# Newton steps for the inverse roots of the expert tiles, constants and FP4 weight loads placed behind tiles, and a permutation inverted in bf16

## The chip, the cores and the metric

The kernel runs on one core of one Trainium2 chip. The metric is the device time in microseconds of one execution. The core has five engines, each with its own queue of instructions that it works off in order: PE (TensorE: matrix products and transposes), DVE (VectorE), ACT (ScalarE), POOL (GpSimd) and SP (SyncE, which here only issues transfers). Engines wait for each other through semaphores. Transfers between HBM and SBUF are issued from the queues of SP, ACT and POOL and are carried out by 16 DMA engines.

## The reference

Six layers work on x, 4 batches of 1024 tokens with 256 features in f32. They form two Macaron blocks; each layer adds its result to x:

```python
x = x + 0.5 * moe(layernorm(x))            # 4 experts, top 1, hidden size 1024
x = x + softmax_attention(layernorm(x))    # 16 heads of 16, causal
x = x + 0.5 * moe(layernorm(x))            # the same weights
x = x + 0.5 * fp4_ffn(layernorm(x))        # hidden size 704
x = x + linear_attention(layernorm(x))     # squared normalised features, running sums
x = x + 0.5 * fp4_ffn(layernorm(x))        # the same weights
```

The two layers that matter here:

```python
def moe(x):
    e = argmax(x @ W_router)                       # one expert per token
    h = gelu(x @ W1[e] + b1[e])
    y = h @ Wo + bo + x
    return (y - mean(y)) * rsqrt(var(y) + 1e-12) * gamma + beta

def fp4_quant_dequant(x):                          # blocks of 16 along the last axis
    scale = max(max(abs(xb)) / 6, 1e-12)
    return nearest of {0, .5, 1, 1.5, 2, 3, 4, 6} to abs(xb / scale), with its sign, times scale

def fp4_ffn(x):
    g, u = q(x) @ q(w_gate).T, q(x) @ q(w_up).T    # q is fp4_quant_dequant
    return q(silu(g) * u) @ q(w_down).T
```

## The kernel before, in words

x stays in SBUF for the whole kernel, as 8 blocks (`xb`) of 512 tokens, that is 128 partitions x 4 x 256. Six stages follow each other. In the profile of before they lie at about 0 to 507 us (MoE, phase 0), 507 to 1580 (softmax attention), 1580 to about 1990 (MoE, phase 1), then FP4, linear attention, and FP4 again until the end.

**Where the order comes from.** The source is written engine by engine, and the program is a trace of it. A scheduler then orders the instructions on each engine by its own estimates of their costs; in the two attention stages parts of PE's order are written out by hand. `tc.keep_in_program_order(ins)` tells the scheduler that `ins` must stand, in its engine's queue, behind everything that the source has given this engine before. It adds no semaphore and no wait of its own; it fixes a place in a queue. Since each queue is worked off in order, an instruction that waits holds back whatever stands behind it on its engine.

**The MoE phase** (`moe_phase`, L247) has three parts.

*Routing* (`moe_route`, L281), for each of the 8 blocks: the block is normalised (`norm_block`, L204: statistics on DVE at L210 and L211, the root on ACT at L213, its reciprocal on DVE at L215, the normalising on ACT at L220), stored to `xn_d` in HBM (L284), transposed on PE (L234) and copied (L235); 8 products with the router's weights give the logits (L292). DVE marks each token's expert in `hot` (L296 to L305), small products give each token's rank (place) among the tokens of its expert (L310 to L325), and then the permutation "token to rank" is turned around. For this the rank is split into a column c and a place q within 128 (L329 to L333). For each group of 128 tokens, `oc` marks the column and `oq` the place, with the token's number in place of a one (L337, L339; f32, 128x128), and the product of the two is summed over all 32 groups into a PSUM bank `inv` (L340). An f32 product is two records on PE. c and q come from adding and subtracting WHOLES = 1.5 * 2^23, which rounds an f32 number to a whole one; `c` keeps WHOLES added, and `alongm` is a row of counting numbers with WHOLES added.

*Plan* (`moe_plan`, L342): `inv` is copied to `invT` (L349); a product of it with a 0/1 matrix `pick` (L380, L382) picks, for each of 38 columns of 128 slots, the tokens to gather (`ids`); `w1_at` gives the rows of the expert's W1 to gather, and `y_at` where each token finds its result.

*Tiles* (`moe_tile`, L415): 19 tiles of 256 slots, each with one expert. POOL issues the gathers: W1 of the expert, 1 MB (L417; three buffers `w1`), and the tokens, two transfers (L422; three buffers `xg`). PE transposes the tokens (L428), ACT copies them (L430), POOL adds the bias bo to `xg` (L432). PE forms the hidden layer in two halves, in PSUM `pairA` and `pairB` (L440), ACT takes the gelu (L447), and PE multiplies by Wo into `acc` (L453). DVE adds `xg` (L456, the first to write y), `norm_block` normalises (L210, L211, L213, L215, L225), POOL multiplies by gamma (`gam0`, halved beforehand at L115) and adds beta (`bet0`, halved at L116) at L458 and L459, and SP stores y to `y_d` (L460). The root at L213 and the gelu at L447 need different tables on ACT, so ACT loads a table on each change between them. There is one `acc` bank; so the next tile's L453 waits until L456 has read it.

After the last tile, each token's result is gathered back and added to x (`give_back`, L274) at the beginning of the next stage.

**Work between the tiles.** `moe_phase` takes a generator `between` and calls `next(between)` after each tile. In phase 0 this is `fp4_weights` (L747): four steps that fill `vas` (128x4096, ones) and `low` (128x512, zeros) on POOL (L749), then 8 parts of w_gate and w_up, and two of w_down. Each part loads `raw` on SP (L755 of 88x512; L773 of 128x352, twice per part), quantises it (`fp4`, L709: L718 to L731 on DVE, with L728 on ACT, and L732 on POOL, which writes `q`), transposes q on PE (L761, L778) and copies the result on ACT (L764). `raw` has two buffers. In phase 1 the generator is empty. The scheduler may move all of this ahead in the queues, and does: the first `raw` is issued at 13.76 us.

**Constants** (L115 to L189): the halving of gam0 and bet0, the identity `ident` and its bf16 copy `ident16` (L122, a cast on DVE), masks for the attention stages (`mask_q`, `keep_kq`, `own`, and `parity` and `row16`, taken from them by DVE at L152 and L154), counting rows (L164, L166), `alongm` (L171), and the `eps` columns that ACT's root takes as a bias (L185, L187).

Of the kernel before, what the change touches and what calls it, by code (L numbers as in the profile page):

```python
# [10 lines left out]
F32 = mybir.dt.float32  # L11
BF16 = mybir.dt.bfloat16
U32 = mybir.dt.uint32
AF = mybir.ActivationFunctionType
# [3 lines left out]
P = 128  # L18
# [24 lines left out]
def macaron_kernel(  # L43
# [38 lines left out]
    def acc_bank(shape):  # L82
        return psum.tile(shape, F32, tag="acc", name="acc", bufs=1)
# [28 lines left out]
    for b in range(2, NBLK):  # L112
        load_x(b)

    nc.gpsimd.tensor_scalar(gam0, gam0, 0.5, None, ALU.mult)  # L115
    nc.gpsimd.tensor_scalar(bet0, bet0, 0.5, None, ALU.mult)  # L116


    ident = const.tile([P, P], F32, tag="ident", name="ident")
    make_identity(nc, ident)  # L120
    ident16 = const.tile([P, P], BF16, tag="ident16", name="ident16")
    nc.vector.tensor_copy(ident16, ident)  # L122
# [4 lines left out]
    nc.gpsimd.memset(mask_q, 0.0)  # L127
    make_causal_mask(nc, mask_q[:, BLK - P :], mask_val=NEG)

    keep_kq = const.tile([P, P], F32, tag="keep_kq", name="keep_kq")  # L130
    nc.gpsimd.memset(keep_kq, 1.0)
    nc.gpsimd.affine_select(
        out=keep_kq, in_=keep_kq, compare_op=ALU.is_ge, fill=0.0, base=0, pattern=[[1, P]], channel_multiplier=-1
    )

    own = const.tile([P, 2, 8, HD + 1], F32, tag="own", name="own")
    nc.gpsimd.memset(own, 1.0)
    for step, base, cm in ((-HD, 0, 1), (HD, HD - 1, -1)):
        nc.gpsimd.affine_select(
            out=own,  # L140
            in_=own,
            compare_op=ALU.is_ge,
            fill=0.0,
            base=base,
            pattern=[[0, 2], [step, 8], [0, HD + 1]],
            channel_multiplier=cm,
        )

    parity = const.tile([P, 2], F32, tag="parity", name="parity")
    own_par = own.rearrange("p g (h two) c -> p g two h c", two=2)  # L150
    for i in range(2):
        nc.vector.tensor_reduce(parity[:, i : i + 1], own_par[:, 0, i, :, 0], AX.X, ALU.add)  # L152
    row16 = const.tile([P, 1], F32, tag="row16", name="row16")
    nc.vector.tensor_reduce(row16, ident.rearrange("p (j c) -> p j c", c=32)[:, :, HD], AX.X, ALU.add)  # L154
# [14 lines left out]
    along = counting("along", [P], 0, [[1, P]], 0)  # L169
    alongm = const.tile([P, P], F32, tag="alongm", name="alongm")  # L170
    nc.vector.tensor_scalar(alongm, along, WHOLES, None, ALU.add)  # L171
    token = counting("token", [TT], 0, [[P, TT]], 1)
# [11 lines left out]
    eps5 = const.tile([P, 1], F32, tag="eps5", name="eps5")  # L184
    nc.gpsimd.memset(eps5, 1e-5)  # L185
    eps12 = const.tile([P, 1], F32, tag="eps12", name="eps12")
    nc.gpsimd.memset(eps12, 1e-12)  # L187
# [10 lines left out]


# [4 lines left out]
    def norm_block(dst, src, eps, last=None):  # L204
# [7 lines left out]
        std = small.tile([P, TPB], F32, tag="std", name="std")  # L212
        nc.scalar.activation(std[:, 0:n], mv[:, 0:n, 1], AF.Sqrt, bias=eps)  # L213
        rstd = small.tile([P, TPB], F32, tag="rstd", name="rstd")
        nc.vector.reciprocal(rstd[:, 0:n], std[:, 0:n])  # L215
# [31 lines left out]
    def moe_phase(tag, between):  # L247
# [4 lines left out]
        with tc.tile_pool(name=f"moe{tag}", bufs=2, reuse_waits="tile") as wp, tc.tile_pool(  # L252
# [6 lines left out]
            inv = acc_bank([P, P])  # L259
# [3 lines left out]
            wf0 = load(f0_wo, "wf0", nc.scalar, sp)  # L263
            for s in range(NE):
                moe_tile(wp, s, xn_d, y_d, wf0, w1_at, ids, b1s)
                next(between, None)
# [14 lines left out]
    def moe_route(wp, b, xn_d, hot, ranks, inv):  # L281
# [48 lines left out]
        nc.vector.tensor_scalar(c, c, WHOLES, None, ALU.add)  # L330
        q = small.tile([P, TPB], F32, tag="q", name="q")
        nc.vector.tensor_scalar(q, c, WHOLES, float(-P), ALU.subtract, ALU.mult)
        nc.vector.tensor_tensor(q, q, r, ALU.add)  # L333
        for i in range(TPB):
            t = b * TPB + i
            oc = wp.tile([P, P], F32, tag="oc", name="oc", bufs=TPB)
            nc.vector.tensor_scalar(oc, alongm, c[:, i : i + 1], None, ALU.is_equal)  # L337
            oq = wp.tile([P, P], F32, tag="oq", name="oq", bufs=TPB)
# [408 lines left out]
    def fp4_weights(wp):  # L747
        for t in (*vas, *low):
            nc.gpsimd.memset(t, 1.0 if t in vas else 0.0)  # L749
            yield  # L750
# [372 lines left out]
```

## Time and profile before

| what | us |
|---|---|
| runs shown | 3208.11, 3191.23, 3205.8 |
| their median | 3205.8 |
| the profiled execution | 3201.22 |
| its span | 3199.5 |
| PE busy | 2630.5 |
| DVE busy | 1565.7 |
| ACT busy | 1036.2 |
| POOL busy | 684.6 |

The profile is of one execution, and its span is the time from the first to the last instruction; 1.7 us of the execution lie around it. Engines work at the same time, so their busy times don't add up to the span. The granted clock of PE, as a share of full speed, is 0.89 in the mean.

In a timeline each row has the start, the time that it took, the engine, the line of the source, the operation, out<-in with the sizes, and how many instructions the row takes together (x4). In brackets stands how long the engine had been idle before, and what it was waiting for. "PEld" is the loading of weights on PE, which runs beside the products. "SPq" and "POOLq" are the issuing of transfers; their time is the engine's, not the transfer's.

The beginning of y (L456) marks the pace of the tiles. Its starts in phase 0, in us: 119.06, 135.51, 158.30, 179.77, 202.47, 223.98, 246.86, 268.24, 289.19, 312.03, 331.81, 348.45, 364.82, 381.20, 397.64, 415.11, 434.26, 450.20, 466.14. In phase 1: 1665.69, 1684.61, 1701.02, 1717.40, 1735.63, 1752.01, 1768.35, 1786.47, 1802.94, 1819.24, 1838.38, 1854.80, 1871.22, 1889.38, 1905.86, 1923.39, 1942.94, 1958.88, 1974.82.

### The profile page before, as it was taken

The page shows a single profiled execution, that of the slowest core. Times are in us where ns is not written, and L with a number is a line of the kernel's source. Part 1 is how long each engine was busy: PE and PEld are TensorE (multiplying, and loading weights), DVE is VectorE, ACT ScalarE, POOL GpSimd, SP SyncE. Part 2 cuts the span into 40 slices and gives each one's busy share as a digit, 9 for nine tenths or more (in the row PEclk, how much of TensorE's full clock was granted, in tenths as well). Part 3 has the DMA queues.
Part 4 walks back from the last instruction along what each step waited for, and adds up shares of the span by engine and source line. Part 5 has one row for each costly group of instructions (what it writes and reads, how often), then busy time and mean ns, then how long its engine had stood idle before and what let it go on. Part 6 is the DMA issues. An engine that isn't in the chain of part 4 may idle for free.

```text
span 3199.5 us, 35882 instructions
## 1 busy us (share of the span) xinstructions
PE 2630.5 (82%) x13697; PEld 1674.4 (52%) x13697; DVE 1565.7 (49%) x3877; ACT 1036.2 (32%) x1704; POOL 684.6 (21%) x760
## 2 busy tenths in 40 slices
PE   6878879998899899899788986678877888777887
PEld 5666754433433343333477775455654555445565
DVE  6233117555445544445231112986446665695644
ACT  3233431333333323333434342233222323232222
POOL 1333323101001001101023342421113322211111
PEclk8789996989889989989869998889988998988898
DMA  4322211000000000000122222100000000000000
GB/s 150 104 75 85 96 41 48 1 1 1 1 1 1 1 1 1 1 1 1 40 96 96 96 86 72 30 7 1 0 0 1 1 1 1 1 7 14 9 12 14
DMA packets 43556, 95.59 MB, mean 30 GB/s; under 512 B 4888, under 2 KB 32056, under 8 KB 38136
## 3 DMA queue, kind: packets, MB, share of 16 engines
q0 software_dynamic: 12192, 58.21, 5.7%
q1 hardware_dynamic: 30280, 32.58, 3.0%
q10 hardware_dynamic: 912, 2.51, 0.3%
q8 instruction: 108, 1.77, 0.2%
q14 instruction: 64, 0.52, 0.1%
HBM read 70.73 MB, written 22.54 MB: 29 GB/s over the span
## 4 chain that ended last, share of the span: by engine, by line
PE 51%; DVE 21%; issue 11%; POOL 7%; DMA 5%; ACT 4%; POOLq 0%; ACTq 0%; DVEq 0%
PE bank L590 11%; PE acc L838 5%; PE acc L652 5%; PE pairA L668 4%; PE bank L565 4%; DMA xg<-xn_d,ids 3%; PE acc L453 3%; POOL hq L732 2%; PE pairA L807 2%; PE pairB L807 2%; DVE sc L965 2%; PE bank L894 2%; DVE part L600 2%; PE pairB L440 1%; PE bank L834 1%
## 5 line engine op out<-in xcount | busy, mean ns | idle before, releaser
L590 PE MATMUL bank<-kT,qT 32*128 32x512 f32 (+3 forms) x1536 | 455.5, 603 | 38.4 <-DVE part L600 18.2
L590 PEld LDWEIGHTS bank<-kT,qT 32*128 32x128 f32 x1536 | 192.8, 206 | 269.4 <-DVE low L605 117.7
L678 ACT ACTIVATE ex<-pairA 128x1024 f32<-128x1024 f32 x192 | 155.5, 810 | 517.3 <-PE bank L590 200.7
L681 POOL TENSOR_SCALAR_AFFINE_SELECT ex<-ex 128x256 f32<-128x256 f32 x256 | 103.3, 408 | 917.4 <-ACT ex L678 913.6
L453 PE MATMUL acc<-wf,gT 128*128 128x256 f32 x1216 | 288.0, 386 | 0.0
L456 DVE TENSOR_TENSOR y<-acc,xg 128x512 f32<-128x512 f32 x38 | 26.3, 692 | 478.7 <-issue 337.9
L453 PEld LDWEIGHTS acc<-wf,gT 128*128 128x128 f32 x1216 | 236.5, 194 | 33.9
L668 PE MATMUL pairA<-qT,kT 32*128 32x512 f32 (+3 forms) x768 | 227.0, 579 | 2.2 <-ACT ex L678 2.2
L838 PE MATMUL acc<-wdT,hqT 128*128 128x256 f32 x768 | 222.0, 448 | 8.2 <-ACT hqT L835 5.4
L600 DVE TENSOR_REDUCE part<-bank 128x1 f32<-128x512 f32 x256 | 168.6, 687 | 76.5 <-PE bank L590 56.9
L668 PE MATMUL pairB<-qT,kT 32*128 32x512 f32 (+3 forms) x768 | 203.0, 576 | 0.0
L838 PEld LDWEIGHTS acc<-wdT,hqT 128*128 128x128 f32 x768 | 170.6, 230 | 50.8 <-ACT hqT L835 22.9
L834 PE MATMUL bank<-ident,hq 128*128 128x128 f32 x384 | 73.5, 345 | 145.7 <-POOL hq L732 145.7
L440 PE MATMUL pairB<-xgT,w 128*128 128x256 f32 x608 | 174.0, 413 | 23.3 <-ACT gT L447 23.3
L605 DVE CUSTOM_DVE_ANT_0 seen<-bank,mask_q 128x128 bf16<-128x128 f32 (+3 forms) x256 | 116.0, 489 | 154.5 <-PE bank L590 147.1
L732 POOL TENSOR_TENSOR hq<-hv,ham 128x1408 f32<-128x1408 f32 x32 | 83.1, 2596 | 496.2 <-DVE hv L731 449.6
L652 PE MATMUL acc<-ex,va 128*32 128x512 f32 (+3 forms) x1536 | 185.4, 550 | 0.9 <-POOL ex L681 0.4
L440 PE MATMUL pairA<-xgT,w 128*128 128x256 f32 x608 | 168.6, 402 | 11.9 <-ACT gT L447 10.5
L807 PE MATMUL pairA<-wgT,xqT 128*128 128x352 f32 x512 | 166.9, 469 | 3.1 <-ACT xqT L235 3.1
L605 DVE CUSTOM_DVE_ANT_0 seen<-bank,mask_q,part 128x128 bf16<-128x128 f32 (+3 forms) x256 | 131.1, 547 | 73.4 <-PE bank L590 62.1
L807 PE MATMUL pairB<-wuT,xqT 128*128 128x352 f32 x512 | 163.1, 461 | 2.6 <-DVE h L817 2.5
L447 ACT ACTIVATE gT<-pairA,b1s 128x256 f32<-128x256 f32 x152 | 71.8, 472 | 276.9 <-PE pairA L440 276.4
(249 smaller groups left out, 4696.0 us busy)
## 6 DMA issues: line engine op xcount, KB each, us to landing
y_d<-y SPq DMA_DIRECT2D x38, 256.0 KB, 2.1
xn_d<-xn SPq DMA_DIRECT2D x16, 512.0 KB, 2.8
x<-in_x SPq DMA_DIRECT2D x8, 512.0 KB, 9.7
out<-x SPq DMA_DIRECT2D x32, 128.0 KB, 1.7
wf<-in_f_wo ACTq DMA_DIRECT2D x2, 1024.0 KB, 9.4
xg<-xn_d,ids POOLq DMA_INDIRECT x76, 2.8
wqk<-in_a_wqk SPq DMA_DIRECT2D x1, 1024.0 KB
back<-y_d,y_at POOLq DMA_INDIRECT x64, 2.7
```

Of the source, the lines that this page charges most:

```text
L440: nc.tensor.matmul(pg[:, f, :], lhsT=w1[:, k * FF + fc * P : k * FF + (fc + 1) * P], rhs=xgT[:, k, :], start=(k == 0), stop=(k == KD - 1),)
L453: nc.tensor.matmul(po[:, j, :], lhsT=gT[fc][:, bass.ts(j, P)], rhs=wf0[:, fc, :], start=(fc == 0), stop=(fc == NF - 1))
L565: nc.tensor.matmul(pp, lhsT=wqk0[:, k, which, g, :], rhs=xnT[:, hb, k, :], start=(k == 0), stop=(k == KD - 1),)
L590: nc.tensor.matmul(pss[j][:, 0:n], lhsT=qT[rows, bass.ts(qt, P)], rhs=kT[rows, c * BLK : c * BLK + n], start=True, stop=True,)
L600: nc.vector.tensor_reduce(part[:, h : h + 1], pss[j][:, 0:n], AX.X, ALU.max, negate=True)
L605: nc.vector.tensor_tensor_reduce(out=seen[:, 0:n], in0=pss[j][:, 0:n], in1=mask_q[:, BLK - n : BLK], scale=-1.0, scalar=part[:, h : h + 1] ...
L652: nc.tensor.matmul(acc[qb][bass.ts(h, 32), c0:BLK], lhsT=va[:, kt, NG * g + h, :], rhs=exs[h // 2][:, h % 2, c0:BLK], start=(kt == 0), sto ...
L668: nc.tensor.matmul(pss[h // 2][:, h % 2, c0:BLK], lhsT=kT[rows, bass.ts(kt, P)], rhs=qT[rows, qb * BLK + c0 : (qb + 1) * BLK], start=True, ...
L678: nc.scalar.activation(ex[:, :, c0:BLK], ps[:, :, c0:BLK], AF.Exp, scale=0.25)
L732: mul.tensor_tensor(dst, v, am.unsqueeze(2).to_broadcast([parts, n, QB]), ALU.mult)
L807: nc.tensor.matmul(pg[:, half, 0:FIH], lhsT=xqT[:, k, bass.ts(i, P)], rhs=w[:, k, half * FIH : (half + 1) * FIH], start=(k == 0), stop=(k ...
L838: nc.tensor.matmul(po, lhsT=hqT[:, c, :], rhs=wdT[:, c, :], start=(c == 0), stop=(c == NFI - 1))
```

## The change

1. *Newton steps.* In the expert tiles, `norm_block` takes the inverse root on DVE by a new function `inverse_roots`: eps is added, a first guess comes from the bits of the number (times -0.5, plus a constant, on its int32 view), and three Newton steps of three operations follow; 11 small DVE operations in all. ACT's root and DVE's reciprocal are left out there. Routing and the other layers keep the root on ACT.
2. *Constants later.* The masks, `parity`, `row16` and the fills of `vas` and `low` move into a generator `later_constants`, from which `fp4_weights` yields first, so that they stand behind tiles 0 to 3, pinned; the fills are on DVE now, not on POOL. `ident16`, `alongm` and `eps12` are gone, `eps5` comes first, and the halving of gam0 and bet0 moves behind the plan of phase 0.
3. *FP4 weights.* The loads of `raw` are pinned on SP, each behind what SP was given before it.
4. *Permutation in bf16.* `oc` and `oq` are bf16. A token's number, up to 4095, is written as two numbers that bf16 holds exactly, the row (0 to 127) and the group (0 to 31), so `oq` is 128x2x128, one product per group of 128 tokens gives both sums, and the plan puts them together (copy, then one DVE operation that adds 128 times the group).
5. *Buffers.* `xg` has four buffers, not three.

The diff, cut (removed lines of constants that appear again in `later_constants` are left out; lines of the file after the change are 37 to 39 higher from `moe_tile` on, so L440 becomes L479, L453 L492, L456 L495, L761 L798 and L778 L815):

```diff
-    nc.gpsimd.tensor_scalar(gam0, gam0, 0.5, None, ALU.mult)
-    nc.gpsimd.tensor_scalar(bet0, bet0, 0.5, None, ALU.mult)
+    eps5 = const.tile([P, 1], F32, tag="eps5", name="eps5")
+    nc.gpsimd.memset(eps5, 1e-5)
...
-    nc.vector.tensor_copy(ident16, ident)
...
-    along = counting("along", [P], 0, [[1, P]], 0)
-    nc.vector.tensor_scalar(alongm, along, WHOLES, None, ALU.add)
-    token = counting("token", [TT], 0, [[P, TT]], 1)
+    along = const.tile([P, P], BF16, tag="along", name="along")
+    nc.gpsimd.iota(along, pattern=[[1, P]], base=0, channel_multiplier=0, ...)
+    token = const.tile([P, TT, 2], BF16, tag="token", name="token")
+    for i in range(2):
+        nc.gpsimd.iota(token[:, :, i], pattern=[[i, TT]], base=0, channel_multiplier=1 - i, ...)
+    row1 = counting("row1", [1], 0, [[1, 1]], 1)
...
+    def later_constants():
+        pinned = tc.keep_in_program_order
+        pinned(nc.gpsimd.memset(mask_q, 0.0))
+        make_causal_mask(nc, mask_q[:, BLK - P :], mask_val=NEG)
+        pinned(nc.gpsimd.memset(keep_kq, 1.0))
...
+        pinned(nc.gpsimd.memset(own, 1.0))
...
+        pinned(nc.vector.tensor_reduce(row16, ident.rearrange("p (j c) -> p j c", c=32)[:, :, HD], AX.X, ALU.add))
+        for t in (*vas, *low):
+            pinned(nc.vector.memset(t, 1.0 if t in vas else 0.0))
+            yield
...
+    def inverse_roots(dst, src, eps):
+        n = src.shape[1]
...
+        nc.vector.tensor_scalar(v, src, eps, None, ALU.add)
+        nc.vector.tensor_scalar(y.bitcast(I32), v.bitcast(I32), -0.5, float(0x5F3759DF), ALU.mult, ALU.add)
+        for step in range(3):
+            nc.vector.scalar_tensor_tensor(u, y, -0.5, y, ALU.mult, ALU.mult)
+            nc.vector.tensor_tensor(u, u, v, ALU.mult)
+            nc.vector.scalar_tensor_tensor(dst if step == 2 else y, u, 1.5, y, ALU.add, ALU.mult)

-    def norm_block(dst, src, eps, last=None):
+    def norm_block(dst, src, eps, last=None, roots=None):
...
+        if roots is nc.vector:
+            inverse_roots(rstd[:, 0:n], mv[:, 0:n, 1], eps)
+        else:
+            std = small.tile([P, TPB], F32, tag="std", name="std")
+            nc.scalar.activation(std[:, 0:n], mv[:, 0:n, 1], AF.Sqrt, bias=eps)
+            nc.vector.reciprocal(rstd[:, 0:n], std[:, 0:n])
...
-            inv = acc_bank([P, P])
+            inv = acc_bank([P, 2, P])
...
         nc.vector.tensor_scalar(c, c, WHOLES, None, ALU.add)
+        nc.vector.tensor_scalar(c, c, WHOLES, None, ALU.subtract)
...
-        nc.vector.tensor_scalar(q, c, WHOLES, float(-P), ALU.subtract, ALU.mult)
-        nc.vector.tensor_tensor(q, q, r, ALU.add)
+        nc.vector.scalar_tensor_tensor(q, c, float(-P), r, ALU.mult, ALU.add)
...
-            nc.vector.tensor_scalar(oc, alongm, c[:, i : i + 1], None, ALU.is_equal)
+            nc.vector.tensor_scalar(oc, along, c[:, i : i + 1], None, ALU.is_equal)
-            oq = wp.tile([P, P], F32, tag="oq", name="oq", bufs=TPB)
-            nc.vector.tensor_scalar(oq, along, q[:, i : i + 1], token[:, t : t + 1], ALU.is_equal, ALU.mult)
+            oq = wp.tile([P, 2, P], BF16, tag="oq", name="oq", bufs=TPB)
+            nc.vector.scalar_tensor_tensor(
+                oq, along.unsqueeze(1).to_broadcast([P, 2, P]), q[:, i : i + 1],
+                token[:, t, :].unsqueeze(2).to_broadcast([P, 2, P]), ALU.is_equal, ALU.mult)
             nc.tensor.matmul(inv, lhsT=oc, rhs=oq, start=(t == 0), stop=(t == TT - 1))
...
-        nc.scalar.copy(invT, inv)
+        nc.scalar.copy(invT, inv[:, 0, :])
+        nc.vector.scalar_tensor_tensor(invT, inv[:, 1, :], float(P), invT, ALU.mult, ALU.add)
...
-        xg = wp.tile([P, nj, D], F32, tag="xg", name="xg", bufs=3)
+        xg = wp.tile([P, nj, D], F32, tag="xg", name="xg", bufs=4)
...
-        norm_block(y, y, eps12)
+        norm_block(y, y, 1e-12, roots=nc.vector)
...
-        for t in (*vas, *low):
-            nc.gpsimd.memset(t, 1.0 if t in vas else 0.0)
-            yield
+        yield from later_constants()
...
-                nc.sync.dma_start(out=raw, in_=src[:, part * 2 * D : (part + 1) * 2 * D])
+                tc.keep_in_program_order(nc.sync.dma_start(out=raw, in_=src[:, part * 2 * D : (part + 1) * 2 * D]))
...
-                nc.sync.dma_start(out=raw, in_=f1_wd[:, a * FI + c0 : a * FI + c0 + FIH])
+                tc.keep_in_program_order(nc.sync.dma_start(out=raw, in_=f1_wd[:, a * FI + c0 : a * FI + c0 + FIH]))
```

## The prediction

> **What bounds the kernel now.** I read the page's totals first, then sums over stretches of time, then the timeline of the stretches that the diff touches.
>
> ```profile
> span 3199.5 us, 35882 instructions
> PE 2630.5 (82%) x13697; PEld 1674.4 (52%) x13697; DVE 1565.7 (49%) x3877; ACT 1036.2 (32%) x1704; POOL 684.6 (21%) x760
> ```
>
> PE is busy for 82% of the span. The two attention stages and the FP4 layers contain no edited instruction, so I ask only about the two MoE phases. The sums by stretch (start:end, length, busy time of each engine, clock):
>
> ```profile
> 200.00:340.00 140.00, 112.32 (x483) 91.35 (x482) 52.30 (x105) 53.67 (x96) 52.73 (x48) 0.91 0.25 82
> 340.00:456.00 116.00, 101.82 (x462) 84.91 (x462) 17.95 (x56) 47.69 (x81) 38.88 (x36) 0.99 0.23 73
> 1642.00:1965.00 323.00, 281.76 (x1248) 234.02 (x1249) 48.50 (x149) 129.83 (x222) 121.98 (x111) 0.95 0.28 92
> ```
>
> The first holds expert tiles with a part of the FP4 weight preparation in each (PE 80%), the second tiles of phase 0 without one (88%), the third the tiles of phase 1 (87%). So PE sets the pace everywhere, and a change pays or costs by the time for which PE stands still. One FP4 tile in detail, on the timeline:
>
> ```profile
> 223.98 0.69 DVE L456 TENSOR_TENSOR y<-acc,xg 128x512 f32<-128x512 f32 x1 [9.16 <-PE acc L453]
> ...
> 225.39 1.28 ACT L213 ACT_TABLE_LOAD   x1
> ...
> 231.01 1.27 POOL L458 TENSOR_TENSOR y<-y,gam 128x512 f32<-128x512 f32 x1
> ...
> 233.98 0.36 SPq L460 DMA_DIRECT2D y_d<-y  x1
> 234.43 0.37 SPq L755 DMA_DIRECT2D raw<-in_f_wu  x1
> ...
> 235.46 2.08 PE L440 MATMUL pairB<-xgT,w 128*128 128x256 f32 x4 [3.16 <-ACT gT L447]
> ```
>
> The reader should see two things. SP takes the store of y 10.0 us after DVE began on it, and a raw FP4 load 0.45 later; this raw is for a part several tiles ahead (the first was issued at 13.76, during routing), so nobody waits for it. And PE's loss is 3.16 us, behind a gelu queued on ACT after an FP4 step.
>
> **The change, part by part.** *Raw loads pinned on SP.* A pinned instruction stands behind all that the program gave its engine before. In the queues of the built program SP now has, for ten tiles: store of y (tile s), raw load, store of y (tile s+1), and so on. DVE has: normalise y of tile s, FP4 of that raw part, y of tile s+1. PE has: the tile's last L492, the transposes of the quantised q (L798, or L815 for wd), and only then the transposes and products of tile s+1. So the whole chain from PE's last product to q lies on PE's path, where before it ran beside it. Step by step, from PE's end as zero:
> - y starts at 0.05; sum and statistics end 1.69 later (223.98 to 225.67): 1.74.
> - Newton: 11 dependent small operations. Those at 64.06, 64.27, 64.47, 64.68 follow each other by 0.205: 2.26. To 4.00. The old way took 1.55 (225.67 to 227.22), so this costs 0.7 here.
> - normalise 0.73; POOL's gamma and beta 1.34 and 1.27 (469.22, 470.56, 471.83): 7.4. Store, then raw 0.45 later: 7.9.
> - raw lands 2.65 after its issue, as the next rows show: 10.6.
>
> ```profile
> 299.28 4.65 SPq L773 DMA_DIRECT2D raw<-in_f_wd  x2
> ...
> 301.93 0.52 DVE L718 TENSOR_REDUCE wam<-raw 128x22 f32<-128x352 f32 x1 [1.13 <-DMA raw<-in_f_wd]
> ```
>
> - FP4 of 88x512: 0.68+0.15+0.35+0.68+0.42 on DVE (40.95 to 43.02), 0.72 on ACT, 0.69+0.69 on DVE, hand-overs 0.4: to 15.3. q on POOL 1.05 (228.38): 16.4.
> - PE then, cold: four transposes 0.8, four of xg 1.09 and 0.68 until the product (1646.45 and 1648.22), the tile's 64 products at 0.2153 each (four follow four by 0.86 from 1656.81 to 1657.67) 13.8, and 1.3 for running at half speed until 1650.9. Period **34.1**.
> - Two wd tiles have two halves, the second load behind the first's landing: 4.06 each (301.93 to 306.0), and q 0.79 (300.88), so q at 19.6, six transposes 1.6, and the same rest: **38.0**.
>
> Ten such intervals: 8 x 34.1 + 2 x 38.0 = 348.8. Before they took 195.2 (the y of tile 4 at 202.47 to that of tile 14 at 397.64): **+153.6**. Bounds: were the chain only 15 at both kinds and PE warm, about 31 x 10: +115; with each DVE step doubled by POOL's traffic, as at 231.51 (1.32 instead of 0.68), 37 x 10 + 8: +183.
>
> The Trainium skill, TensorE: Matmul & The Clock Gate, section "HAM oscillation — how this bites in real kernels", says that a gap of about 3.4 us in PE's work drops its clock to half, so that work split by gaps is paid for twice, once in the gap and again in the warm-up; this speaks against a change that makes ten gaps. The trace agrees in kind: after 3.16 us of idle at 235.46 four products took 2.08 and 1.91 until 240.7. By the page's 3.4 us of warm-up a gap would lose some 1.7 us (an estimate), 4 us more over ten than my row's 1.3.
>
> *Square root by Newton steps, and a fourth xg buffer.* Two table loads of 1.28 (225.39 and 227.00) and the root of 0.30 leave ACT in each of 38 tiles, and with them the gelu that stands behind them. Tiles of phase 1 start y every 16.4 us (1684.61, 1701.02, 1717.40), every third 18.2. Their products alone are 13.8; 2.6 of the rest is the loads. In the built queues tiles without FP4 now come in pairs, with transposes of two or three tiles together: 13.8 then 13.8 + 8 or 10 x 0.18 (0.55 for three, 229.16) = 15.2 to 15.6, or 14.85 where two transposes and the copy of 0.68 come between. Phase 0: tiles 0 to 4 58.05 instead of 83.4 (119.06 to 202.47), **-25.4**; tiles 14 to 18 57.75 instead of 68.5, **-10.7**. Phase 1: 18 intervals of 261.4 instead of 309.1; as gelus and gathers will hold PE now and then I take **-45**. Bounds: nothing gained if the gathers of w set the 16.4, so 0, and -47.7 - 36.1 = -83.8; I take -81.1, being near the end that counts PE's own records. At each phase's last tile, nothing covers the Newton chain: 2.26 + 467.84 against 468.40, **+1.7** twice.
>
> *Masks, fills, identity.* In the first 26 us:
>
> ```profile
> 14.64 8.18 DVE L122 CAST ident<-ident 128x128 bf16<-128x128 f32 x1
> ...
> 14.85 6.97 POOL L749 MEMSET va<- 128x4096 f32 x2
> ...
> 25.77 2.16 PE L234 MATMUL bank<-ident,xn 128*128 128x128 f32 x8 [20.45 <-ACT xn L220]
> ```
>
> DVE's cast stood for 8.18 beside POOL's fills, and the first transposes waited until 25.77. Both are gone from there; ACT no longer waits for eps until 14.66. DVE's reciprocal of block 0 still stands behind the statistics of block 2, whose x lands at 13.58: transposes at about 15.8, **-9.9** (bounds -12 and 0, if something else on POOL is late). The fills move to DVE behind tiles 0 to 3, 8 x 0.69 = 5.5 for 128x4096 at a 128x512 operation's rate, in at least 9 us of DVE idle per tile (9.16 above): 0; uncovered the four fills would be 12.4 in all. The masks go to POOL there (3.1, from 10.65 to 13.71) and are read only from 507: 0.
>
> *Inversion in bf16.* Per block 4 products of 128x256 in one pass replace 4 of 128x128 f32, two records each (0.77 for two at 68.33, 69.18 among the route's own products). Two of the four stand before the next block's route: 0.3 to 0.72 saved. DVE's operations, oq now of twice the width (0.34 to between 0.34 and 0.69), lie in 3.7 us of idle per block (70.64). 8 blocks: **-5** in phase 0 and **-4.5** in phase 1 (bounds -12 and 0 each); the plan's added operation, 0.35, is inside. Moving the halving of gam0 and bet0 (0.86 + 0.85, POOL, 8.76) past the plan puts it into the 26 us between first gather (92.75) and first y (119.06), which POOL spends mostly in issues: 0, or at most +1.7.
>
> Sum: -9.9 - 5 - 25.4 + 153.6 - 10.7 + 1.7 = +104.3 in phase 0; -4.5 - 45 + 1.7 = -47.8 in phase 1; **+56.5**. The profiled execution took 3201.2 (span 3199.5 and 1.7 around it), so 3257.7; the median of the runs shown is 3205.8, 4.6 above that execution, so **3262**.
>
> **The rivals.**
> - *Slower still*: the stalls come, and the pairs gain nothing in either phase because gathers of w (1 MB a tile, 92 GB/s in phase 1) set the period: 3262 + 81 = 3343. For it: w has three buffers still. Against: PE waits in those stretches are behind ACT.
> - *Faster*: FP4 runs a tile ahead off PE's path, raw being issued before PE ends its tile. Then the ten tiles take about 15.4 (13.8, eight transposes, a little for gelus), 154 instead of 195.2: 56.5 - 194.8 = -138, so 3067. It decides where raw is issued 16 us or more before PE's last product; the pin puts it 7.9 after.
> - *No change*: SP lets raw past the waiting store, but DVE's order stays, so the chain ends at 10.7 instead of 16.4: 10 x -5.8 = -58, 3204. Against: in before SP's raw follows the store by 0.45 at 234.43, 257.01 and 278.31.
>
> **How the numbers follow.** Forecast 0.82, slower still 0.08, faster 0.05, no change 0.05. Half a per cent, 16 us, is about what a measurement of this kernel can tell from no change. Slower 0.90, same 0.05, faster 0.05. The forecast's own spread, from the bounds of the stall (-38 and +29), the pairs and the start, is 3225 to 3300; up towards the slower rival I reach to 3310.
>
> **What would show it.** Right: in ten tiles of phase 0 PE idles 16 to 20 us before L798 or L815, released by POOL, and y comes every 34 to 38 us there; raw issues 0.45 after the store; no table load between gelus; phase 1's tiles 45 us shorter; first transposes near 16; fills of va on DVE inside tiles. Wrong: raw issued ahead of its store, y less than 30 us apart in these tiles, or 16.4 kept in phase 1.

## The result, and the profile after

The changed kernel takes 3291.7 us (median; 3287.8 to 3299.3), the kernel before 3207.0 beside it: 1.027 times as long, 95% interval 1.0215 to 1.0321. The forecast was 3262.

First the page's totals of the changed kernel, then its sums by stretch (columns as before): the ten tile intervals with FP4 parts, the four intervals after them, and the eighteen of phase 1.

```profile
span 3288.1 us, 36102 instructions
PE 2618.5 (80%) x13633; PEld 1661.2 (51%) x13633; DVE 1628.1 (50%) x4260; ACT 936.7 (28%) x1589; POOL 678.1 (21%) x757
```

```profile
169.84:530.67 360.83, 181.09 (x732) 149.16 (x733) 83.00 (x264) 58.05 (x115) 79.72 (x74) 0.72 0.16 50
530.67:588.45 57.78, 56.88 (x266) 47.87 (x264) 17.57 (x72) 18.13 (x36) 16.82 (x14) 1.00 0.13 42
1801.51:2061.81 260.30, 258.87 (x1220) 219.13 (x1218) 83.14 (x324) 78.77 (x162) 110.41 (x98) 1.00 0.29 94
```

The totals hardly differ from before: PE 82% then, 80% now. The stretches show what they hide. PE is busy for 50% of the FP4 stretch (80% before), and for 98% and 99% of the other two (88% and 87% before). So the change left PE almost no idle time in most tiles, and half of the time idle in ten intervals. One of the ten on the timeline:

```profile
205.34 0.69 DVE L495 TENSOR_TENSOR y<-acc,xg 128x512 f32<-128x512 f32 x1 [19.84 <-PE acc L492]
...
209.24 0.73 DVE L252 TENSOR_SCALAR y<-y,mv,rstd 128x256 f32<-128x256 f32 x2
...
211.39 1.26 POOL L498 TENSOR_TENSOR y<-y,bet 128x512 f32<-128x512 f32 x1
212.68 0.38 SPq L499 DMA_DIRECT2D y_d<-y  x1
213.15 0.36 SPq L792 DMA_DIRECT2D raw<-in_f_wg  x1
216.11 0.68 DVE L757 TENSOR_REDUCE wam<-raw 88x32 f32<-88x512 f32 x1 [6.14 <-DMA raw<-in_f_wg]
...
220.91 1.05 POOL L771 TENSOR_TENSOR q<-wv,wam 88x512 f32<-88x512 f32 x1 [8.25 <-DVE wv L770]
...
222.02 0.85 PE L798 MATMUL bank<-ident,q 88*128 88x88 f32 x4 [16.77 <-POOL q L771]
...
224.39 2.08 PE L479 MATMUL pairA<-xgT,w 128*128 128x256 f32 x4 [0.68 <-ACT xgT L469]
```

The start, on the same timeline:

```profile
16.03 2.17 PE L261 MATMUL bank<-ident,xn 128*128 128x128 f32 x8 [10.52 <-ACT xn L247]
```

PE's first transposes come at 16.03 (25.77 before), as forecast. The tile above is the chain of the forecast, link by link: the store 0.03 after POOL's last operation (211.39 + 1.26), raw 0.47 behind the store, DVE idle for 6.14 until raw lands, and PE idle for 16.77 until q is there. The next y follows at 240.08, so this interval is 34.74 long. The other signs came too: from the first to the last y of phase 0 ACT loads one table instead of 37, and the fills of va lie on DVE inside tiles (3.47 each, at 123.48 and 133.61).

All times by stage, in us. "To first y" is routing, plan and the first tile; tiles are counted from 0, from y to y; "softmax" runs from its first transposes to those of phase 1's routing.

| kernel | first transposes | to first y | tiles 0-4 | 4-14 | 14-18 | last y to softmax | softmax | to first y, phase 1 | tiles of phase 1 | rest |
|---|---|---|---|---|---|---|---|---|---|---|
| before | 25.8 | 93.3 | 83.4 | 195.2 | 68.5 | 19.7 | 1090.4 | 89.5 | 309.1 | 1224.7 |
| after | 16.0 | 95.8 | 58.0 | 360.8 | 57.8 | 23.0 | 1098.1 | 92.0 | 260.3 | 1226.3 |
| loads free | 16.3 | 103.1 | 59.1 | 159.8 | 57.8 | 23.0 | 1088.3 | 90.5 | 260.3 | 1222.7 |
| pins alone | 25.7 | 92.3 | 66.1 | 347.1 | 69.1 | 19.7 | 1106.3 | 92.3 | 309.4 | 1221.4 |
| one step ahead | 15.8 | 93.9 | 59.0 | 214.6 | 58.0 | 23.0 | 1087.5 | 91.8 | 260.3 | 1229.4 |
| f32 inversion | 16.1 | 92.8 | 58.2 | 360.9 | 58.0 | 23.0 | 1087.4 | 92.5 | 262.1 | 1227.7 |
| late start | 15.8 | 95.7 | 64.5 | 161.1 | 57.8 | 23.0 | 1086.3 | 92.1 | 260.3 | 1229.8 |
| root on ACT, loads free | 15.9 | 102.8 | 72.4 | 186.3 | 67.2 | 19.8 | 1111.3 | 91.7 | 303.9 | 1221.2 |
| FP4 order pinned | 16.1 | 93.7 | 58.0 | 314.1 | 58.0 | 23.0 | 1106.4 | 91.7 | 260.3 | 1227.4 |
| fills late alone | 18.4 | 93.9 | 84.7 | 198.5 | 68.7 | 19.7 | 1098.7 | 90.5 | 313.4 | 1221.2 |
| loads free, f32 | 16.6 | 94.6 | 59.3 | 159.8 | 58.2 | 23.0 | 1102.6 | 88.0 | 262.0 | 1228.9 |
| loads free, f32, relu on DVE | 16.5 | 96.5 | 58.2 | 150.1 | 58.2 | 23.1 | 1091.3 | 92.5 | 262.3 | 1222.1 |

A caution for reading it: the softmax stage has nearly the same instructions in all twelve kernels, yet it takes 1086 to 1111 us in these profiles, and PE's busy time and granted clock go with it. The sums over that stage, the first of the kernel with a late start, the second of the one with the root on ACT:

```profile
418.00:1504.00 1086.00, 975.67 (x5503) 412.48 (x5504) 542.70 (x1654) 372.83 (x526) 125.45 (x278) 0.91 0.01 4
```

```profile
464.30:1575.60 1111.30, 1001.32 (x5504) 429.82 (x5505) 544.43 (x1659) 374.84 (x529) 125.70 (x279) 0.88 0.01 4
```

The counts agree, PE's busy time differs by 25.6 us, and the clock is 0.91 and 0.88. So single executions can differ by some 25 us in this stage alone, and effects of a few us are read from the other stages, not from whole times. Each row of the table is one execution.

### The profile page after: what moved, and what is told of

It reads as the page before. It is cut to its first block, busy times and chain, and to the rows that moved or that the text cites. A ratio compares the mean times of both kernels' runs of the same rounds, so it can differ in the third digit from the quotient of the medians.

```text
span 3288.1 us, 36102 instructions
## 1 busy us (share of the span) xinstructions
PE 2618.5 (80%) x13633; PEld 1661.2 (51%) x13633; DVE 1628.1 (50%) x4260; ACT 936.7 (28%) x1589; POOL 678.1 (21%) x757
## 4 chain that ended last, share of the span: by engine, by line
PE 61%; DVE 22%; issue 5%; POOL 5%; ACT 4%; DMA 3%; SPq 0%; POOLq 0%; another core or an unknown queue 0%; ACTq 0%; DVEq 0%
PE bank L629 10%; PE acc L492 7%; PE acc L875 5%; PE acc L691 5%; PE pairA L479 4%; PE pairB L479 4%; PE pairA L707 4%; PE bank L604 3%; PE pairA L844 2%; POOL hq L771 2%; PE pairB L844 2%; DVE sc L1002 2%; DVE part L639 2%; PE bank L931 2%; PE bank L871 2%
## 5 line engine op out<-in xcount | busy, mean ns | idle before, releaser
L492 PE MATMUL acc<-wf,gT 128*128 128x256 f32 x1216 | 268.7, 379 | 0.0
L495 DVE TENSOR_TENSOR y<-acc,xg 128x512 f32<-128x512 f32 x38 | 26.2, 690 | 478.9 <-PE acc L492 249.1
L492 PEld LDWEIGHTS acc<-wf,gT 128*128 128x128 f32 x1216 | 231.0, 190 | 31.4
L479 PE MATMUL pairA<-xgT,w 128*128 128x256 f32 x608 | 175.6, 415 | 10.4 <-ACT xgT L469 9.6
L479 PE MATMUL pairB<-xgT,w 128*128 128x256 f32 x608 | 167.8, 401 | 0.0
L717 ACT ACTIVATE ex<-pairB 128x1024 f32<-128x1024 f32 x192 | 154.6, 805 | 2.1 <-PE pairB L707 1.1
```

The lines of the kernel that those rows point to most:

```text
L479: nc.tensor.matmul(pg[:, f, :], lhsT=w1[:, k * FF + fc * P : k * FF + (fc + 1) * P], rhs=xgT[:, k, :], start=(k == 0), stop=(k == KD - 1),)
L492: nc.tensor.matmul(po[:, j, :], lhsT=gT[fc][:, bass.ts(j, P)], rhs=wf0[:, fc, :], start=(fc == 0), stop=(fc == NF - 1))
L717: nc.scalar.activation(ex[:, :, c0:BLK], ps[:, :, c0:BLK], AF.Exp, scale=0.25)
```

## The experiments

### The loads of raw free again

```diff
-                tc.keep_in_program_order(nc.sync.dma_start(out=raw, in_=src[...]))
+                nc.sync.dma_start(out=raw, in_=src[...])
...
-                tc.keep_in_program_order(nc.sync.dma_start(out=raw, in_=f1_wd[...]))
+                nc.sync.dma_start(out=raw, in_=f1_wd[...])
```

> The changed kernel, with the loads of raw no longer pinned on SP; all else as in the change. Theory (raw issued behind the tile's own store puts the whole chain norm, store, load, FP4, q on PE's path): raw goes ahead in SP's queue, q is ready before PE asks, and the ten intervals from the y of tile 4 to that of tile 14 fall from 360.8 us to about 157 to 165 (13.8 of products, 0.7 of token transposes, 0.5 of q's transposes, 0.7 to 1.5 for the copies on ACT); the time falls by about 200, to 3085 to 3100. Rival (Newton steps or DVE's order of FP4 behind the normalising hold PE, the load adds only its 2.65 + 0.45 per part): the intervals fall by about 31, to 330, and the time to about 3260. Tiles 0 to 4, 14 to 18 and phase 1 stay within 2 us of 58.0, 57.8 and 260.3 by both.

3084.5 us, 0.964 times before (0.9606 to 0.9674). The ten intervals fell from 360.8 to 159.8; tiles 0-4 are 1.1 longer, the other two as they were. One tile of it:

```profile
194.50 0.47 PE L798 MATMUL bank<-ident,q 88*128 88x88 f32 x4
...
199.28 0.32 SPq L792 DMA_DIRECT2D raw<-in_f_wu  x1
...
200.94 1.13 PE L479 MATMUL pairB<-xgT,w 128*128 128x256 f32 x4 [0.98 <-ACT gT L486]
```

PE takes q without idling, since it is of a part worked on earlier, and raw is issued in the middle of a tile for the next one. The only wait left is 0.98 for a gelu. Without the two pins the change is worth -3.6% instead of +2.7%: the pins were the loss, and the rival as it was put (ten intervals of about 330 us with the loads free) falls. But with the loads free the scheduler moved FP4 on DVE ahead too, so this run doesn't tell whether the load's own latency or FP4's place on DVE held PE; a later run does. Not foreseen: two FP4 parts went into the routing, which took 7.3 us more to the first y.

### The pins alone, in the kernel before

```diff
-                nc.sync.dma_start(out=raw, in_=src[...])
+                tc.keep_in_program_order(nc.sync.dma_start(out=raw, in_=src[...]))
...
-                nc.sync.dma_start(out=raw, in_=f1_wd[...])
+                tc.keep_in_program_order(nc.sync.dma_start(out=raw, in_=f1_wd[...]))
```

> The kernel before, with nothing but the two pins on the loads of raw added. Theory: the ten stalls come without Newton steps too; from tile 4 to tile 14 some 340 to 360 us instead of 195.2, tiles 0 to 4 fall from 83.4 to about 66 (no FP4 part beside them any more), tiles 14 to 18 and phase 1 as before (68.5 and 309.1); in all +125 to +145, about 3340. Rival (the stalls need the change's other parts, Newton's longer chain or the pairs of tiles): within 30 us of before, 3207 to 3235.

3348.3 us, 1.0454 times before (1.0403 to 1.0506). Tiles 4-14 took 347.1, tiles 0-4 66.1, phase 1 309.4, all as the theory had it. In one of the ten intervals, whose y began at 252.83:

```profile
258.63 0.36 SPq L460 DMA_DIRECT2D y_d<-y  x1
259.09 0.37 SPq L755 DMA_DIRECT2D raw<-in_f_wg  x1
...
267.85 0.85 PE L761 MATMUL bank<-ident,q 88*128 88x88 f32 x4 [15.12 <-POOL q L732]
```

It is the same chain, 15.0 us from y to q; with Newton's steps it takes 16.7 to 17.0. The pins need no other part of the change to make these stalls. Alone they cost 152 us in tiles 4-14 (347.1 against 195.2), and 17 come back in tiles 0-4, which have no FP4 part any more. In the changed kernel they cost 201 there (360.8 against 159.8), since its intervals without the stall are 35 shorter (159.8 against 195.2) and those with it 14 longer.

### Pinned, but one step ahead

```diff
+        def fetch():
+            if sources:
+                rows, src = sources.pop(0)
+                raw = wp.tile([P, 2 * D], F32, tag="raw", name="raw")[0:rows, 0 : src.shape[1]]
+                tc.keep_in_program_order(nc.sync.dma_start(out=raw, in_=src))
+                raws.append(raw)
+        for i, _ in enumerate(later_constants()):
+            if i == 3:
+                fetch()
+            yield
...
-                raw = wp.tile([P, 2 * D], F32, tag="raw", name="raw")[0:r]
-                tc.keep_in_program_order(nc.sync.dma_start(out=raw, in_=src[...]))
+                fetch()
+                raw = raws.pop(0)
```

> The changed kernel with the loads of raw still pinned on SP, but each issued one step earlier: part 0 behind tile 3, and part k+1 before part k is worked on. Theory (it is the distance between load and use, not the pin): raw waits in SBUF, DVE works on it right after normalising the tile before, q is there some 11 us after the start of a tile whose products take 13.8, PE doesn't wait; ten intervals of 15.7 to 17, 157 to 170 in all instead of 360.8; time 3085 to 3105. Rival (any place behind a store on SP costs a stall, because the store waits for POOL): the intervals stay above 300 and the time above 3230.

3139.2 us, 0.981 (0.9779 to 0.9846): most of the loss is gone, but the ten intervals took 214.6, not 157 to 170, and the time lies above the expected 3085 to 3105. From the timeline of one tile, whose y began at 187.56:

```profile
196.32 0.36 SPq L499 DMA_DIRECT2D y_d<-y  x1
...
196.77 0.37 SPq L796 DMA_DIRECT2D raw<-in_f_wg  x1
...
200.12 0.68 DVE L757 TENSOR_REDUCE wam<-raw 88x32 f32<-88x512 f32 x1 [6.53 <-DMA raw<-in_f_wg]
...
206.02 0.85 PE L812 MATMUL bank<-ident,q 88*128 88x88 f32 x4 [3.05 <-POOL q L771]
```

The scheduler used the step won to move FP4 a tile ahead too, so DVE still waits for a load that was just issued. The chain from y to q is now 18.5 us (187.56 to 206.02), and a tile's products cover some 15.4 of it; PE waits for 3.05. It does so in every second of the eight w_gate and w_up intervals (2.4 to 4.3 us); the half speed after a wait makes the next tile long enough to cover the chain. I had counted DVE as free to take a raw already there. The two w_down steps still took 35.0 and 32.5:

```profile
323.42 0.36 SPq L499 DMA_DIRECT2D y_d<-y  x1
323.83 4.70 SPq L796 DMA_DIRECT2D raw<-in_f_wd  x2
...
331.24 1.12 PE L829 MATMUL bank<-ident,q 128*128 128x128 f32 x4 [13.88 <-POOL q L771]
```

Such a step takes two loads and this edit issues one ahead, so the load of its second half still stands behind the store of its own tile (at 323.83 here, at 358.68 in the second step), and PE waits for 13.88 and 14.98. So the distance decides, as the theory had it, and one tile is 3 us too short.

### The inversion back in f32

```diff
-            oc = wp.tile([P, P], BF16, tag="oc", name="oc", bufs=TPB)
-            nc.vector.tensor_scalar(oc, along, c[:, i : i + 1], None, ALU.is_equal)
-            oq = wp.tile([P, 2, P], BF16, tag="oq", name="oq", bufs=TPB)
...
+            oc = wp.tile([P, P], F32, tag="oc", name="oc", bufs=TPB)
+            nc.vector.tensor_scalar(oc, alongm, c[:, i : i + 1], None, ALU.is_equal)
+            oq = wp.tile([P, P], F32, tag="oq", name="oq", bufs=TPB)
+            nc.vector.tensor_scalar(oq, along, q[:, i : i + 1], token[:, t : t + 1], ALU.is_equal, ALU.mult)
...
-        xg = wp.tile([P, nj, D], F32, tag="xg", name="xg", bufs=4)
+        xg = wp.tile([P, nj, D], F32, tag="xg", name="xg", bufs=3)
```

> The changed kernel with the inversion of the permutation in f32 as before, and three xg buffers instead of four (f32 takes the room of the fourth). The change's routing took 95.8 us from the first transposes to the first y in phase 0 and 92.0 in phase 1, before 93.3 and 89.5, where I had forecast 5 less. Theory A (the shorter bf16 products leave PE idle for more of the routing, its clock stays lower, and the added operation and DVE's wider oq lengthen the plan): 93.3 and 89.5 come back, within 1 us. Theory B (the new order of constants and DVE's queue did it): 95.8 and 92.0 stay. For the buffers: if the fourth gave the pairs of tiles their pace, phase 1's 18 intervals rise from 260.3 towards 270 or more; if it is the Newton steps alone, they stay at 260 to 262.

One execution: 3280.4. To the first y it took 92.8 in phase 0, as theory A asks, but 92.5 in phase 1, as theory B asks; neither holds. By blocks of the routing (starts of the first DVE operation behind the logits) bf16 does what I had priced: a block takes 7.27 us in the changed kernel and 8.10 in f32, 0.83 less. But only four of its seven intervals are that short; one is 9.45, because PE reaches the inversion's products before DVE has made oq, and f32 has one of 6.35. In the block of 9.45, PE's first product waits for oq, and the three behind it for 0.19 each:

```profile
38.54 0.37 PE L378 MATMUL acc<-oq,oc 128*128 128x256 bf16 x1 [0.89 <-DVE oq L370]
```

From the last block to the first y, bf16 takes 35.6 against 32.0. Of these 3.6, 1.7 lie before the transposes of the first tile's tokens: the gather of the tokens starts 9.5 us after the block's first operation instead of 7.8, behind an operation of DVE's later in the plan (L446) and not behind the tokens' numbers. The other 1.9 lie in the first tile, where two more groups of products ran at half speed (1.91 and 1.85 us, in f32 1.03); two other bf16 kernels, one step ahead and FP4's order pinned, took 33.7 and 33.6 without that. Over all kernels with no FP4 in the routing, bf16 took 93.7 to 95.8 and f32 92.3 and 92.8 to the first y; in phase 1 bf16 90.5 to 92.1 and f32 88.0 to 92.5. So the inversion gains nothing in phase 0, loses 1 to 3 us in these executions, and in phase 1 no difference can be told. The buffers: with three, phase 1's intervals take 262.1 instead of 260.3, so the Newton steps carry nearly all of that gain.

### A late start, then free loads

The first load is pinned behind the store of tile 0; the later ones are free.

```diff
+        def fetch(pin=lambda ins: ins):
...
+                pin(nc.sync.dma_start(out=raw, in_=src))
...
+        for i, _ in enumerate(later_constants()):
+            if i == 0:
+                fetch(tc.keep_in_program_order)
+            yield
```

> The changed kernel with only the first load of raw pinned on SP, behind the store of tile 0; each later load is free and is given one step ahead, as in the run with one step ahead. Without any pin two FP4 parts went into the routing, which then took 103.1 us to the first y instead of 95.8. Theory (the pin has one use, to keep FP4 out of the routing): 94 to 96 us to the first y; the two parts go into tiles 0 to 4, which take 59 to 63; tiles 4 to 14 stay at 158 to 162; time 3074 to 3084. Rival (the load's pin costs wherever it stands): tiles 0 to 4 or 4 to 14 grow by 15 us or more, time above 3090.

3088.2 us, 0.9617 (0.9575 to 0.9658), 4 above the expected range. The routing came back to 95.7, but tiles 0-4 took 64.5, a little over the 59 to 63 expected: two intervals of 17.4 and 19.5 hold the first parts. What was won in the routing was mostly given back, and by its time it can't be told from the kernel with all loads free. This one pin, which is not behind the store of the tile that uses its load, cost little.

### The root on ACT again, loads free

```diff
-        norm_block(y, y, 1e-12, roots=nc.vector)
+        norm_block(y, y, eps12)
```

> The changed kernel with no pins on the loads of raw and the expert tiles' roots on ACT again; four xg buffers stay. Theory (the table loads around each root hold the gelus, and these PE): phase 1's 18 intervals go back from 260.3 to 305 to 312, tiles 14 to 18 from 57.8 to 66 to 69, time 3160 to 3180. Rival (the fourth buffer or the order in pairs gave it): phase 1 below 275, time below 3110.

One execution: 3194.2. Phase 1 took 303.9 (1.1 less than expected) and tiles 14-18 67.2, with four xg buffers still there: the Newton steps give the gain of the plain tiles. The whole time is 14 above the range, since tiles 0-14, which I had not listed, also lost 40 us (72.4 and 186.3 against 59.1 and 159.8), and the softmax stage took the 1111 us shown above. The way from the last y to the softmax stage fell from 23.0 to 19.8.

### Raw early, FP4's place on DVE kept

```diff
-        nc.vector.tensor_reduce(am, src, AX.X, ALU.max, apply_absolute_value=True)
+        first = nc.vector.tensor_reduce(am, src, AX.X, ALU.max, apply_absolute_value=True)
+        if tag == "w":
+            tc.keep_in_program_order(first)
```

The loads of raw are free in this kernel.

> The changed kernel with loads of raw free on SP, but the first FP4 operation of each part (the block maxima) pinned on DVE, so that each part still stands behind the normalising of its tile, and only the store and the load leave the chain. Theory (the stall is a sum: normalising 4.7, gamma, beta and store up to the load 3.2, landing 2.7, FP4 4.8, q 1.1): the intervals fall by the 5.8 of the store and load, to 28 to 30 for w_gate and w_up and 30 to 33 for w_down, 285 to 310 in all instead of 360.8; time 3215 to 3240. Rival (the transfer alone is the stall, DVE's order is harmless once raw is there): 160 to 180 in all, time below 3110.

One execution: 3250.4, 10 above the range with the softmax stage at 1106. The ten intervals took 314.1, 4 above it, each w_gate or w_up interval 30.7 to 31.3. One of them:

```profile
203.70 0.68 DVE L757 TENSOR_REDUCE wam<-raw 88x32 f32<-88x512 f32 x1
...
204.41 0.75 DVE L760 TENSOR_SCALAR wam<-wam 88x32 f32<-88x32 f32 x1
...
205.58 1.43 DVE L764 TENSOR_TENSOR wv<-raw,wrs 88x512 f32<-88x512 f32 x1
...
210.91 0.85 PE L800 MATMUL bank<-ident,q 88*128 88x88 f32 x4 [11.86 <-POOL q L773]
```

DVE begins FP4 right behind the normalising, without waiting for raw, and PE still waits for 11.86. So the stall's parts add up nearly as priced: store and load are worth 4.7 an interval (46.8 in all, where I had said 5.8 each). What is missing is on DVE: two FP4 operations that now lie beside POOL's gamma and beta take 0.75 and 1.43, and took 0.18 and 0.69 in the changed kernel (at 216.83 and 217.43), behind POOL's operations. The sums over the ten intervals, here and then with the loads free:

```profile
167.82:481.89 314.07, 183.14 (x730) 149.91 (x731) 95.72 (x265) 57.95 (x115) 79.73 (x74) 0.73 0.17 57
```

```profile
178.44:338.25 159.81, 151.94 (x725) 126.27 (x724) 69.70 (x244) 52.27 (x111) 78.56 (x72) 1.00 0.34 108
```

Of the other 154 us between 314.1 and 159.8, PE is idle for 123 (130.9 against 7.9), behind DVE's and POOL's work, and busy for 31 longer, at a clock of 0.73 instead of 1.00. The rival (the transfer alone) falls. The pin's harm is that the load pulls FP4 behind the tile's end; its own latency is a quarter of it.

### The fills late, in the kernel before

```diff
-            nc.gpsimd.memset(t, 1.0 if t in vas else 0.0)
+            tc.keep_in_program_order(nc.gpsimd.memset(t, 1.0 if t in vas else 0.0))
```

> The kernel before with nothing but the four fills of va and low pinned on POOL behind the tiles whose step they are. Theory (DVE's cast of 8.18 us is slow only because POOL fills at the same time): the cast takes some 0.2, the first transposes start at 16.5 to 18 instead of 25.8. Rival (the cast is slow by itself, or eps, ready at 14.6 on POOL behind the masks, sets the start): the cast stays above 5 us, or the first transposes stay after 22. The time as a whole: 8 us less by the start, 2 to 4 back where the fills lie between gathers in the tiles; 3195 to 3205.

One execution: 3209.4, 4 above the range. The cast that took 8.18 before:

```profile
14.54 0.38 DVE L122 CAST ident<-ident 128x128 bf16<-128x128 f32 x1
```

With POOL's fills moved away it takes 0.38, and the first transposes start at 18.4 instead of 25.8, 0.4 after the range. So 7.4 of the 9.7 us won at the start belong to the fills. Left on POOL between the gathers they cost 1.3 in tiles 0-4 (one interval of 25.45), and the whole time shows no gain.

### Free loads with the f32 inversion, and then the relu on DVE

```diff
-        nc.scalar.activation(m, m, AF.Relu, bias=halves[0:parts], scale=HALVES)
+        if tag == "w":
+            nc.vector.tensor_scalar(m, m, HALVES, -HALVES, ALU.mult, ALU.add)
+            nc.vector.tensor_scalar(m, m, 0.0, None, ALU.max)
+        else:
+            nc.scalar.activation(m, m, AF.Relu, bias=halves[0:parts], scale=HALVES)
```

The first of the two kernels has free loads, the inversion in f32 and three xg buffers; the second also this edit.

> The changed kernel with free loads of raw and the inversion in f32 as before, with three xg buffers. In the run with free loads alone, two FP4 parts lay in the routing, which took 103.1 us to the first y; in the kernel before they lay there too, and it took 93.3. Theory (in bf16 PE's inversion products stand where they wait for DVE's oq, and FP4 on DVE makes these late; in f32 the routing covers FP4): 92 to 95 us to the first y. Rival (the two parts cost it whatever the inversion): 100 to 104. Tiles 0 to 4 about 59, 4 to 14 about 160, phase 1 262; time by the theory 3070 to 3082, by the rival 3080 to 3090.

> The same as the run with free loads and f32, and the one FP4 operation on ACT (the relu between two DVE operations) taken to DVE as two operations, for the weights alone. With free loads, the tiles with FP4 take 16.15 us each, since gelus stand behind that relu on ACT and PE waited 0.98 for one. Theory: without it ten intervals fall from 160 to 150 to 154, time 6 to 10 below the run without this edit, 3062 to 3076. Rival (DVE, with two operations more, or the copies set the pace): the ten intervals stay at 158 or more.

The first: 94.6 to the first y against 103.1 (the second 96.5), so with two FP4 parts in the routing the f32 inversion is the better one (the other bf16 kernel with them, the root on ACT, took 102.8); but 3100.5 in all (0.963, 0.9561 to 0.9702; single times from 3069 to 3108), above the expected range, with 1102.6 in the softmax stage. The second: the ten intervals fell from 159.8 to 150.1, 14.95 each, as the theory said; 3082.1 us, 0.9611 (0.9566 to 0.9657), above the expected 3062 to 3076. The wait of gelus behind ACT's FP4 step was the last one in these tiles: PE is busy for 149.1 of the 150.1 us. Four versions without the harmful pins thus beat both kernels, the one before by 3.6 to 3.9%; among the four the whole times decide nothing.

## Why the prediction was right, and where its sizes were off

| term | forecast | measured |
|---|---|---|
| start, to the first transposes | -9.9 | -9.7 |
| routing and plan, phase 0 | -5 | +2.5 |
| tiles 0 to 4 | -25.4 | -25.4 |
| tiles 4 to 14 | +153.6 | +165.7 |
| tiles 14 to 18 | -10.7 | -10.7 |
| last tile to the softmax stage | +1.7 | +3.3 |
| softmax stage | 0 | +7.7 |
| routing and plan, phase 1 | -4.5 | +2.5 |
| tiles of phase 1 | -45 | -48.8 |
| from phase 1's last y to the end | +1.7 | +1.6 |
| sum | +56.5 | +88.6 |

The mechanism was right: a load pinned behind its own tile's store puts the chain to q on PE's path, ten times, and outweighs gains of 95 us elsewhere. It was read from the queues of the built program and priced from rows of the trace; the first two experiments show it from both sides, and the run with FP4's order pinned shows its parts. The price of the plain tiles in phase 0 was right to 0.1 us. That PE's own records set it was right; the 0.1 is in part luck, since a pair of tiles had been priced at 28.65 to 29.4 (measured 28.9 and 29.1). In phase 1 my allowance of 3 us for gelus and gathers was not needed. One reading was wrong without harm: the raw issued at 234.43 in the kernel before was not for a part several tiles ahead, but for the next one, which DVE began at 252.38, 18 us later. That no one waited for it is right.

Four terms were mis-sized.

*The stall, +12.1.* The two w_down intervals took 38.0 and 37.9, as forecast; the eight others 35.6 in the mean instead of 34.1. q was late by only 0.5 (16.8 to 17.1 us after PE's end instead of 16.4). The rest is PE's half speed, which I took as 1.3 us an interval from one row. It is 2.6 in the mean, and it alternates. PE in the next of the ten intervals:

```profile
256.79 0.85 PE L798 MATMUL bank<-ident,q 88*128 88x88 f32 x4 [16.81 <-POOL q L771]
...
262.74 1.91 PE L479 MATMUL pairA<-xgT,w 128*128 128x256 f32 x4
264.45 1.32 PE L479 MATMUL pairB<-xgT,w 128*128 128x256 f32 x4
265.61 1.03 PE L479 MATMUL pairA<-xgT,w 128*128 128x256 f32 x4
```

Four products take 1.91 at half speed and 1.03 at full. Here half speed lasts from 256.79 to about 265.0, 8.2 us, and from the first product of the tile to its y it takes 17.05 us (259.17 to 276.22) where 13.85 would do: 3.2 lost. In the interval before it lasted from 222.02 to about 227.5, 5.5 us, and 1.8 were lost (224.39 to 240.08, 15.69). The Trainium skill (TensorE: Matmul & The Clock Gate, section "What's actually happening") gives about 3.4 us of sustained work before PE is at full speed again. The 1.7 a gap that I had estimated from it were nearer than my own row, and both are low: half speed lasted longer here.

*The inversion, +7.5 and +7.0.* The step that failed is "two of the four stand before the next block's route: 0.3 to 0.72 saved". The saving exists (0.83 in each of four blocks of phase 0), but it was given back where PE meets its products before oq is made (one block of 9.45 against 6.35), in the plan (1.7), and in the first tile, where PE stayed at half speed for longer (1.9, in this execution). I had looked for DVE's idle time in the block, and not at where in PE's queue the products stand; and I had no term for the plan's reordered DVE queue beyond 0.35. In phase 1, bf16's 90.5 to 92.1 show that the forecast's gain didn't come, and not why: f32 alone varies from 88.0 to 92.5 there.

*The last tile, +1.6.* Every kernel with Newton steps takes 23.0 from the last y to the softmax stage, every one without 19.7 to 19.8. Newton's chain is 1.6 of these 3.3 (forecast 1.7); the rest is DVE's queue, where the first block's reciprocal now stands behind two more additions of tokens coming back (610.61 in the changed kernel).

*The softmax stage, +7.7.* Four kernels with the changed constants and Newton steps took 1086 to 1088 there, three others 1091, 1103 and 1106. It goes with the clock of the execution, and no experiment ties it to the change.

Of the rivals, "slower still" is excluded by phase 1, where the gathers of w set nothing (99% PE). "Faster" is what the kernel does once the pins are gone: 159.8 for the ten intervals against my 154, and 3084.5 against 3067; the routing took 103.1 where the forecast had 88.3. "No change" was priced as raw issued early with DVE's order kept: 58 less than the forecast; the experiment with FP4's order pinned gave 47.

## What to carry to other kernels

Before pinning a transfer in a queue, write down what stands ahead of it there, what that waits for, and how long after it the first user asks; if the chain from there to the user is longer than the work that covers it (here 18.5 against 15.4 us even one tile ahead), the difference is paid each time, with PE's half speed after the wait on top (1.8 to 3.2 us a tile here). An average of busy time can stay the same while most stages gain and one is ruined, so compare stage by stage. A faster instruction pays only from the place that its queue gives it: the bf16 products were shorter and the routing was not.

## What the runs showed of the hardware that was not expected

- A DVE cast of 128x128 to bf16 took 8.18 us beside POOL's fills and 0.38 without them; it ended with the first two fills (6.97 from 14.85) and the two small ones behind them, and everything behind it on DVE waited. The Trainium skill (SBUF — State Buffer, section "SBUF: two separate sides") says that a DVE operation in a two-port mode and a GpSimd operation take a shared port pair as a lock: the one that starts first has it for its whole instruction, and the other is blocked. The two runs agree with a lock, and show that it held over four POOL instructions in a row. Which ports the cast used no run shows, and by its record it had begun 0.21 before the first of these fills.
- After about 16.9 us of idle PE ran at half speed for 5.5 to 6.4 us in five intervals and for 8.1 to 8.2 in three, in turn from the second of them on (intervals of 34.7 to 35.5 and of 36.1 to 36.5 in the changed kernel; with the pins alone, after some 15.3 us of idle, all eight w_gate and w_up intervals but the first took 34.0 to 34.2). What sets which was not tried.
- Nearly the same softmax stage took 1086 to 1111 us in the twelve kernels, one execution each, with the granted clock at 0.91 to 0.88.
